# Layer 1 of a two-layer graph network: seven weights of interleaving moved from the slice steps to the scan, and two small products moved ahead of the decay's

## The chip, the cores and the metric

The kernel runs as one program on one NeuronCore of a Trainium2 chip. The metric is the device time of one execution in microseconds (us). The time before is 4291.2 us, the median of three runs (4290.76 to 4305.48 us). The profile was taken from one further execution.

## The reference, cut to what matters

`x` is 32 graphs of 512 nodes with 256 features, `adj` their adjacency. Two layers run one after the other. Layer 0 and the fall-back path of the kernel are not touched by the change. Layer 1 is an attention over the graph, and then a token mixer:

```python
# --- layer 1 ---
x = x + _L1_gnn_ref(_layernorm(x), adj, ...)      # graph attention, 4 heads of 64
x = x + _L1_ffn_ref(_layernorm(x), ...)           # slices, scan, un-slicing

# inside _L1_ffn_ref, for each graph:
sw = softmax((xm @ W_slice.T + b_slice) / temp)   # 512 nodes x 8 heads x 64 slices
st = einsum('bhnc,bhng->bhgc', fx, sw) / (sw.sum(2) + 1e-05)   # 64 slice tokens of 512
ot = _hydra(st, ...)                              # two-way scan over the 64 tokens
out = einsum('bhgc,bhng->bhnc', ot, sw)           # back to the nodes
return out @ out_w.T + out_b

# inside _hydra: z, xBC, dt from one projection; a 3-tap convolution and silu on xBC;
# y = forward and backward scan with decay exp(dt * A), moved by one token, plus
y = y + x_og * repeat(x_og @ fcD_w.T + Dp, P)     # the skip
yg = y * silu(z);  yg = yg * rsqrt(mean(yg**2) + 1e-05) * norm_w
return yg @ out_w.T
```

## The kernel before, in words

**Two streams.** `layer1_plain` writes layer 1 as Python generators. `attentions()` gives the attention of all 32 graphs in small steps: `prepare` (gather of x, layer norm, transposes, the product `hp`, the rows `own`), `attention` (the tiles `att` on VectorE, then the products `avp` and `adp` on TensorE, then the transposes `dp` and `bp`), and `norm` (the head-wise layer norm of the result, called from within the next graph's attention). `mixer(g)` gives the token mixer of a pair of graphs: `slices` for each graph, `tokens`, `scan` for both together, `unslice` for each graph.

**How they are woven.** The last loop draws values from `mixer`. Each `yield n` adds n times `PACE` to a credit, and for each whole credit one step of `attentions()` is called there. `PACE` is 1.04 * 2 * (14 + 12) / 68 = 0.795, and the weights of one pair sum to 68 before and after. The weights so decide where in the mixer's program text the attention of later graphs stands. A scheduler then sorts the instructions of each engine by the program's order and by its own view of what is ready, so that a step need not end up exactly where it was called. Each engine runs its list in order.

**The scan's chain, with its lines.** `xp` L1402 (TensorE) is evicted to `xpad` L1406 (ScalarE). VectorE runs the convolution: twelve instructions for `xT` (L1418, L1420), then `sp` (L1428 to L1434), then three for `bcT` (L1418, L1420). ScalarE makes `cpad` from it (L1445). TensorE's `gp` L1491 waits for `cpad`. The step sizes `sp` go on through L1461 to L1471 to `seg` L1485 on VectorE, for which `segp` L1495 on TensorE waits. ScalarE makes `decay` from it (L1497), and VectorE multiplies it into `mix` (L1514). `xtp` L1500 (transposes of x) and `qp` L1505 (the skip's product) need only `xT`; VectorE's `dq` L1507 reads `qp`. `yp` L1521 needs `mix`. Then come `yTp` L1531, its copy L1533 (ScalarE), `oTp` L1539, its copy L1542, `vp` L1559, and `outp` L1569 with the additions L1571 (VectorE) in `unslice`.

**The slices' chain.** `x4T` transposes, `lgp` L1336 (TensorE), exponential L1337 (ScalarE), softmax L1338 to L1343 (VectorE), then `yTp` L1348 and the transposes `swp` L1353 on TensorE.

**The norm's chain.** `mu` L1294 to L1300 on VectorE, then one power L1301 on GpSimd, then `av` L1304 and the addition L1305 on VectorE. GpSimd's list also holds the gathers L1149 (four for each graph, each pair's first waiting until a tile of x has been written out), `short` L1087, the powers L30 and L31 of the layer norms, and the additions L947 and L1187.

Of the kernel before, what the change touches and what calls it, by code (L numbers as in the profile page):

```python
# [13 lines left out]
AF = mybir.ActivationFunctionType  # L14
# [8 lines left out]
NT = N // P  # L23
# [841 lines left out]
def layer1_plain(tc, ident, eps, x2s, ranks, adj, w, out, over, ps):  # L865
# [3 lines left out]
    nc = tc.nc  # L869
    B = adj.shape[0]  # L870
    SEG = B // len(x2s)
    GB = 2
# [4 lines left out]
    G = w["W_slice"].shape[0]  # L877
# [23 lines left out]
    with ExitStack() as ctx:  # L901
# [3 lines left out]
        def ctile(name, shape):  # L905
            return cst.tile(shape, F32, tag=name, name=name)
# [6 lines left out]
        def psum(tag, name):  # L913
            return ps.tile([P, N], F32, tag=tag, name=name)
# [8 lines left out]
        with tc.tile_pool(name="raw0", bufs=1, side="right") as raw:  # L923
# [12 lines left out]
            for c in range(DC):  # L936
                nc.tensor.matmul(pn[:, : 2 * AH], ones, norm2[:, c].rearrange("p i h -> p (i h)"),
                                 start=c == 0, stop=c == DC - 1)
# [6 lines left out]
        def add_rows(xt, i):  # L945

            nc.gpsimd.dma_start(xt.rearrange("p t d -> p (t d)"), added[i].partition_broadcast(P), accum_op=ALU.add)  # L947
# [31 lines left out]
        seg_l, seg_r, side = ctile("seg_l", [P, G]), ctile("seg_r", [P, G]), ctile("side", [P, 2, G])  # L979
# [126 lines left out]
        def inner(name):  # L1106
            return sb.tile([P, DI], F32, tag="inner", name=name, bufs=6)
# [8 lines left out]
        def normed(xt, xn, name):  # L1116

            mv = sb.tile([P, NT, 2], F32, tag="mv" + name[0], name=f"mv{name}")
            for t in range(NT):
                st = sb.tile([P, 6], F32, tag="st" + name[0], name=f"st{name}_{t}", bufs=4)  # L1120
                nc.vector.bn_stats(st, xt[:, t, :])
                nc.vector.bn_aggr(mv[:, t, :], st)
            rs = sb.tile([P, NT], F32, tag="rs" + name[0], name=f"rs{name}")
            deviation(nc, rs, mv[:, :, 1], eps)
            shift = sb.tile([P, NT], F32, tag="shift" + name[0], name=f"shift{name}")
            nc.vector.scalar_tensor_tensor(shift, mv[:, :, 0], -1.0, rs, ALU.mult, ALU.mult)
            for t in range(NT):
                nc.scalar.activation(xn[:, t, :], xt[:, t, :], AF.Identity, bias=shift[:, t : t + 1],
                                     scale=rs[:, t : t + 1])

        def turned(xn, tag, name, want=None):

            xnT = sb.tile([P, DC, N], F32, tag=tag, name=name, bufs=1)
            for c in range(DC):
                pt = psum("any", f"{name}p{c}")
                for t in range(NT):
                    nc.tensor.transpose(pt[:, t * P : (t + 1) * P], xn[:, t, c * P : (c + 1) * P], ident)
                nc.scalar.copy(xnT[:, c, :], pt)  # L1138
                if c + 1 < DC:
                    yield want  # L1140
            return xnT
# [177 lines left out]
        def slices(b, j, yT, rn):  # L1319


            while b not in attended:
                next(ahead)
            xt = xs[b]
            xn = sb.tile([P, NT, D], F32, tag="xn", name=f"x4{b}", bufs=1)
            normed(xt, xn, f"d{b}")
            yield 5
            xnT = yield from turned(xn, "x4T", f"x4T{b}", 1)
            add_rows(xt, 1)
            sw = sb.tile([P, NT, DI], F32, tag="sw", name=f"sw{b}", bufs=1)  # L1330
            swT = sb.tile([P, KC, N], F32, tag="swT", name=f"swT{b}")
            yield 2
            for t in range(NT):
                pf = psum("any", f"lgp{b}_{t}")
                for c in range(DC):
                    nc.tensor.matmul(pf, xnT[:, c, t * P : (t + 1) * P], wsl[:, c, :], start=c == 0, stop=c == DC - 1)  # L1336
                nc.scalar.activation(sw[:, t, :], pf, AF.Exp)  # L1337
                nc.vector.tensor_mul(sw[:, t, :], sw[:, t, :], ebsl)  # L1338
                s = sw[:, t, :].rearrange("p (h g) -> p h g", h=H)
                st = sb.tile([P, H], F32, tag="sst", name=f"sst{b}_{t}")  # L1340
                nc.vector.tensor_reduce(st, s, AX.X, ALU.add)  # L1341
                nc.vector.reciprocal(st, st)
                nc.vector.tensor_mul(s, s, st.unsqueeze(2).to_broadcast([P, H, G]))  # L1343
                yield 5 if t + 1 == NT else 1
            for c in range(DC):
                py = psum("any", f"yTp{b}_{c}")
                for t in range(NT):
                    nc.tensor.matmul(py, xn[:, t, c * P : (c + 1) * P], sw[:, t, :], start=t == 0, stop=t == NT - 1)  # L1348
                nc.scalar.copy(yT[:, c, :, j, :], py.rearrange("p (h g) -> p h g", h=H))
            for k in range(KC):  # L1350
                pt = psum("any", f"swp{b}_{k}")
                for t in range(NT):
                    nc.tensor.transpose(pt[:, t * P : (t + 1) * P], sw[:, t, k * P : (k + 1) * P], ident)  # L1353
                nc.scalar.activation(swT[:, k, :], pt, AF.Identity, accum_out=rn[:, j, k : k + 1])
            nc.vector.tensor_scalar_add(rn[:, j, :], rn[:, j, :], 1e-5)
            nc.vector.reciprocal(rn[:, j, :], rn[:, j, :])
            return swT
# [26 lines left out]
        def scan(g, uT):  # L1384
# [4 lines left out]
            def chunks(t):  # L1389
                return t.rearrange("p (k n) -> p k n", k=KC)  # L1390
# [8 lines left out]
            for k in range(KC):  # L1399
                for c in range(KC):  # L1400
                    x0 = 2 * H + DI + k * P
                    nc.tensor.matmul(px[:, k * T : (k + 1) * T], inT[:, c, x0 : x0 + P], uT[:, c, :],  # L1402
                                     start=c == 0, stop=c == KC - 1)
# [70 lines left out]
            def heads(t):  # L1474
                return t.rearrange("p (h l) -> p h l", h=H)

            def per_head(a):
                return a.unsqueeze(2).to_broadcast([P, H, G])

            def per_slice(a):  # L1480
                return a.unsqueeze(1).to_broadcast([P, H, G])

            seg = [inner(f"seg{g}_{j}") for j in range(GB)]
            for j in range(GB):
                nc.vector.tensor_mul(heads(seg[j]), per_head(la[:, j, :]), per_slice(seg_r))  # L1485
            yield 7

            pg = psum("any", f"gp{g}")
            for i in range(2):
                for j in range(GB):  # L1490
                    nc.tensor.matmul(pg[j * G : (j + 1) * G, i * G : (i + 1) * G], bcT[:S, j, :],  # L1491
                                     cpad[:, j, 2 * i : 2 * i + G], start=True, stop=True)
            pl = psum("any", f"segp{g}")
            for j in reversed(range(GB)):
                nc.tensor.matmul(pl[j * G : (j + 1) * G, :], seg_l, seg[j], start=True, stop=True)  # L1495
            decay = inner(f"decay{g}")
            nc.scalar.activation(decay, pl, AF.Exp)  # L1497
            pt = psum("any", f"xtp{g}")
            for k in range(KC):
                nc.tensor.transpose(pt[:, k * P : (k + 1) * P], chunks(xT)[:, k, :], ident)  # L1500
# [2 lines left out]
            pq = psum("any", f"qp{g}")  # L1503
            for c in range(KC):
                nc.tensor.matmul(pq[:, :H], chunks(xT)[:, c, :], fcT[:, c, :], start=c == 0, stop=c == KC - 1)  # L1505
            q = sb.tile([P, H], F32, tag="dq", name=f"dq{g}")
            nc.vector.tensor_add(q, pq[:, :H], skip)  # L1507
            gm = sb.tile([P, 2, G], F32, tag="gm", name=f"gm{g}", bufs=1)
# [4 lines left out]
            nc.vector.tensor_add(mix, mix, back)  # L1513
            nc.vector.tensor_mul(mix, mix, decay)  # L1514

            yield 7
            py = psum("any", f"yp{g}")
            for h in range(H):
                for j in range(GB):
# [5 lines left out]
            nc.vector.tensor_add(y, y, py)  # L1525
            nc.vector.tensor_mul(y, y, z)
            ms = sb.tile([P, 1], F32, tag="ms", name=f"ms{g}")
            yield 5
            pt = psum("any", f"yTp{g}")
            for k in range(KC):  # L1530
                nc.tensor.transpose(pt[:, k * P : (k + 1) * P], y[:, k * P : (k + 1) * P], ident)  # L1531
            yT = inner(f"yT{g}")
            nc.scalar.copy(yT, pt)  # L1533
            nc.scalar.activation(z, y, AF.Square, accum_out=ms)
            yield 2
            po = psum("any", f"oTp{g}")
            for k in range(KC):
                for c in range(KC):
# [8 lines left out]
                    nc.vector.tensor_scalar(rms[i * G : (i + 1) * G, j : j + 1], ms[j * G : (j + 1) * G], 1.0 / DI, LN_EPS,  # L1547
                                            ALU.mult, ALU.add)
            nc.gpsimd.tensor_tensor(rms, rms, eps[:, 1:2].to_broadcast([P, GB]), ALU.pow)
            yield 2  # L1550

            v = sb.tile([P, NT, DI], F32, tag="sw", name=f"v{g}", bufs=1)
            v = v.rearrange("p t d -> p (t d)").rearrange("p (j k d) -> p j k d", j=GB, k=KC)
# [10 lines left out]
        def unslice(b, swT, v):  # L1564
            xt = xs.pop(b)
            for t in range(NT):
                po = psum("any", f"outp{b}_{t}")
                for k in range(KC):
                    nc.tensor.matmul(po[:, :D], swT[:, k, t * P : (t + 1) * P], v[:, k, :],  # L1569
                                     start=k == 0, stop=k == KC - 1)  # L1570
                nc.vector.tensor_add(xt[:, t, :], xt[:, t, :], po[:, :D])  # L1571
            nc.sync.dma_start(out[b].rearrange("(t p) d -> p t d", p=P), xt)
            stored.add(b)

        def mixer(g):
            uT = sb.tile([P, KC, GB * G], F32, tag="uT", name=f"uT{g}", bufs=1)
            yT = sb.tile([P, DC, H, GB, G], F32, tag="yT", name=f"yT{g}", bufs=1)
            rn = sb.tile([P, GB, KC], F32, tag="rn", name=f"rn{g}")
            sws = []
            for j in range(GB):  # L1580
                sws.append((yield from slices(g * GB + j, j, yT, rn)))
            yield 3
            tokens(g, yT, rn, uT)
            v = yield from scan(g, uT)
            yield 2
            for j in range(GB):
                unslice(g * GB + j, sws[j], v[:, j])
                yield 2


        ahead = attentions()
# [649 lines left out]
```

## Time and profile before

| | us |
|---|---|
| runs | 4305.48, 4290.76, 4291.2 (median 4291.2) |
| the profiled execution, its own time | 4294.7 |
| its span, first to last instruction | 4293.0 |
| TensorE busy | 3772.2 (88%) |
| VectorE busy | 3183.1 (74%) |
| ScalarE busy | 2105.0 (49%) |
| GpSimd busy | 1576.3 (37%) |
| first `xp` (scan of the first pair) | starts at 2498.9 |
| last `xp` (scan of the sixteenth pair) | starts at 4226.7 |

Layer 0 fills the first half of the span. From about 2400 us on only layer 1 runs, and from the first `xp` on one pair of graphs follows the other. Busy time is the time in which an engine has an instruction; matmuls are pipelined, so that a busy TensorE is not one at its peak. A row of the timeline gives start, time to the last end, engine, line, operation, output and inputs, and the count of merged records; in square brackets stands the idle time before it and what ended it. One matmul of the program is two records or more there. "PEclk" is the granted clock of TensorE as a share of full speed.

### The profile page before, as it was taken

What the parts mean: (1) busy time and instruction counts of PE and PEld (TensorE: products, weight loads), DVE (VectorE), ACT (ScalarE), POOL (GpSimd) and SP (SyncE); (2) the same over time, 40 slices, a digit from 0 to 9 for tenths busy, and PEclk for the clock granted to TensorE, in tenths of its full rate; (3) what the DMA queues carried; (4) which work ended last, traced back from release to release, by engine and by line L of the source; (5) the groups of instructions that cost most, each with busy time, mean ns of one, the idle gap of its engine ahead of it and who ended that gap; (6) DMA issues with size and microseconds to landing.
All of it is one profiled execution on the core that took longest, in us unless ns stands there. A gap on an engine that the chain in (4) does not pass through costs nothing. (4 is left out here: it accounts for less than half of the span.)

```text
span 4293.0 us, 54585 instructions
## 1 busy us (share of the span) xinstructions
PE 3772.2 (88%) x19031; PEld 2392.6 (56%) x19031; DVE 3183.1 (74%) x6973; ACT 2105.0 (49%) x4260; POOL 1576.3 (37%) x1973
## 2 busy tenths in 40 slices
PE   5567998989999999888998789999999999999997
PEld 4454565665655666554555255555555555555555
DVE  6668877888778987777775777777777777777663
ACT  3344655556556666555665344444443444444432
POOL 2345643564435644354332322223222223222210
PEclk8778999999999999999999899999999999999998
DMA  4557654575546754386542332323322333232210
GB/s 131 166 159 223 192 164 138 174 222 158 161 135 186 222 165 138 115 266 190 160 145 66 82 74 71 75 64 79 69 71 73 79 79 79 65 74 65 60 30 16
DMA packets 313244, 523.95 MB, mean 122 GB/s; under 512 B 104535, under 2 KB 196324, under 8 KB 312957
## 3 DMA queue, kind: packets, MB, share of 16 engines
q0 software_dynamic: 129408, 383.06, 32.1%
q1 hardware_dynamic: 183548, 137.29, 10.9%
q8 instruction: 152, 2.49, 0.2%
q14 instruction: 136, 1.11, 0.1%
HBM read 463.10 MB, written 73.95 MB: 125 GB/s over the span
## 5 line engine op out<-in xcount | busy, mean ns | idle before, releaser
L623 PE MATMUL clsp<-xnT,wc 128*128 128x512 f32 x1024 | 517.2, 623 | 35.0 <-ACT cls L625 30.7
L623 PE MATMUL gatep<-xnT,wg 128*128 128x512 f32 x1024 | 498.5, 606 | 19.7 <-ACT gate L625 19.6
L652 PE MATMUL po<-wd,acc 128*128 128x256 f32 x2048 | 455.4, 381 | 6.4 <-DVE acc L641 5.2
L652 PEld LDWEIGHTS po<-wd,acc 128*128 128x128 f32 x2048 | 388.9, 191 | 72.8 <-issue 9.8
L1211 DVE SCALAR_TENSOR_TENSOR att<-own,other,mask 128x512 f32<-128x512 f32 x512 | 364.5, 741 | 61.6 <-DMA own<-ownd 60.2
L599 DVE SCALAR_TENSOR_TENSOR best<-rows,xs,best 128x1024 f32<-128x1024 f32 x212 | 271.2, 1281 | 128.0 <-ACT best L593 70.0
L637 DVE SCALAR_TENSOR_TENSOR acc<-past,fld,acc 128x512 f32<-128x512 f32 x448 | 332.8, 745 | 28.8 <-ACT past L636 20.6
L623 PEld LDWEIGHTS gatep<-xnT,wg 128*128 128x128 f32 x1024 | 196.5, 196 | 262.0 <-issue 199.8
L632 ACT ACTIVATE acc<-tz,fld 128x512 f32<-128x512 f32 x256 | 199.1, 778 | 276.9 <-PE tz L630 247.0
L596 POOL DMA_INDIRECT rows<-table,xs x212 | 258.4, 1219 | 181.7 <-DVE best L599 114.3
L636 ACT ACTIVATE past<-tz,fld 128x512 f32<-128x512 f32 x448 | 291.0, 695 | 68.0 <-DVE acc L637 67.2
L1248 PE MATMUL avp<-att,hv 128*32 128x512 f32 x2048 | 260.7, 611 | 26.7 <-DVE att L1211 26.7
L1149 POOL DMA_INDIRECT x<-x2s,ranks x128 | 151.9, 1186 | 344.2 <-DVE x L1571 128.5
L623 PEld LDWEIGHTS clsp<-xnT,wc 128*128 128x128 f32 x1024 | 182.0, 198 | 169.4 <-issue 111.5
L435 PE MATMUL pm<-h,adj 128*128 128x258 f32 (+1 forms) x1024 | 180.0, 322 | 100.1 <-DVE keep L428 37.7
L1348 PE MATMUL yTp<-sw,x 128*128 128x512 f32 x512 | 242.0, 613 | 28.3 <-DVE sw L1343 28.0
L554 POOL DMA_INDIRECT xs<-rows_of,order x128 | 158.3, 1237 | 264.1 <-DVE acc L637 98.4
L625 ACT ACTIVATE gate<-gatep,fld 128x512 f32<-128x512 f32 x256 | 175.8, 687 | 156.3 <-PE gatep L623 133.8
L1301 POOL TENSOR_TENSOR mu<-mu,eps 128x16 f32<-128x16 f32 x32 | 112.0, 3499 | 361.5 <-DVE mu L1300 361.4
L1336 PE MATMUL lgp<-wsl,x4T 128*128 128x512 f32 x512 | 239.1, 610 | 1.9 <-ACT x4T L1138 1.8
L1569 PE MATMUL outp<-v,swT 128*128 128x256 f32 x1024 | 227.7, 380 | 0.0
L435 PEld LDWEIGHTS pm<-h,adj 128*128 128x128 f32 x1024 | 150.4, 211 | 124.6 <-issue 73.5
(580 smaller groups left out, 8227.4 us busy)
## 6 DMA issues: line engine op xcount, KB each, us to landing
adj<-in_adj POOLq DMA_DIRECT2D x128, 256.0 KB, 5.1
x<-added POOLq DMA_DIRECT2D x64, 512.0 KB, 5.2
own<-ownd SPq DMA_DIRECT2D x128, 256.0 KB, 3.7
rows_of<-keep SPq DMA_DIRECT2D x32, 550.0 KB, 3.9
x<-in_x SPq DMA_DIRECT2D x32, 512.0 KB, 5.3
xs<-bd POOLq DMA_DIRECT2D x32, 512.0 KB, 6.2
x2s<-xs SPq DMA_DIRECT2D x32, 512.0 KB, 2.9
short<-in_adj POOLq DMA_DIRECT2D x32, 512.0 KB, 6.0
```

The source lines that it names most:

```text
L435: nc.tensor.matmul(pm[:, : c1 - c0], a[:, i, t * P : (t + 1) * P], h[:, i, c0:c1], start=i + c0 == 0, stop=i + 1 == NT and c0 > 0)
L596: nc.gpsimd.indirect_dma_start(out=row, out_offset=None, in_=table, in_offset=bass.IndirectOffsetOnAxis(ap=idxs[:, k : k + 1].bitcast(U32) ...
L599: nc.vector.scalar_tensor_tensor(m, row, vals[:, k : k + 1], m, ALU.add, ALU.max)
L623: nc.tensor.matmul(pf, wf[:, c, f * P : (f + 1) * P], xnT[:, c, :], start=c == 0, stop=c == DC - 1)
L636: nc.scalar.activation(r, z, AF.Relu, bias=fld[:, f, AT + b : AT + b + 1])
L637: nc.vector.scalar_tensor_tensor(y, r, fld[:, f, CH + b : CH + b + 1], y, ALU.mult, ALU.add)
L652: nc.tensor.matmul(po[:, i, :], acc[f][:, t * P : (t + 1) * P], wd[:, f, :], start=f == 0, stop=f == FC - 1)
L1211: nc.vector.scalar_tensor_tensor(e, own[h], other[:, j, h : h + 1], mask[:, j, :], ALU.max, ALU.mult)
L1248: nc.tensor.matmul(pv[p][k * HW : (k + 1) * HW, :], hv[:, j, h, e : e + HW], weighed[b, h, j], **ends)
L1336: nc.tensor.matmul(pf, xnT[:, c, t * P : (t + 1) * P], wsl[:, c, :], start=c == 0, stop=c == DC - 1)
L1348: nc.tensor.matmul(py, xn[:, t, c * P : (c + 1) * P], sw[:, t, :], start=t == 0, stop=t == NT - 1)
L1569: nc.tensor.matmul(po[:, :D], swT[:, k, t * P : (t + 1) * P], v[:, k, :], start=k == 0, stop=k == KC - 1)
```

## The change

Seven of the 68 weights per pair are taken from `slices` (three in each of two graphs) and `unslice` (one) and given to `scan`. In `scan`, the transposes `xtp` with their copy and the product `qp` are written ahead of `segp` and `decay`. No instruction is added or removed.

```diff
@@ slices @@
             normed(xt, xn, f"d{b}")
-            yield 5
+            yield 3
...
-                yield 5 if t + 1 == NT else 1
+                yield 4 if t + 1 == NT else 1
@@ scan @@
                 nc.vector.tensor_mul(heads(seg[j]), per_head(la[:, j, :]), per_slice(seg_r))
-            yield 7
+            yield 9
 
             pg = psum("any", f"gp{g}")
...
-            pl = psum("any", f"segp{g}")
-            for j in reversed(range(GB)):
-                nc.tensor.matmul(pl[j * G : (j + 1) * G, :], seg_l, seg[j], start=True, stop=True)
-            decay = inner(f"decay{g}")
-            nc.scalar.activation(decay, pl, AF.Exp)
             pt = psum("any", f"xtp{g}")
...
             for c in range(KC):
                 nc.tensor.matmul(pq[:, :H], chunks(xT)[:, c, :], fcT[:, c, :], start=c == 0, stop=c == KC - 1)
+            pl = psum("any", f"segp{g}")
+            for j in reversed(range(GB)):
+                nc.tensor.matmul(pl[j * G : (j + 1) * G, :], seg_l, seg[j], start=True, stop=True)
+            decay = inner(f"decay{g}")
+            nc.scalar.activation(decay, pl, AF.Exp)
             q = sb.tile([P, H], F32, tag="dq", name=f"dq{g}")
...
             nc.vector.tensor_mul(mix, mix, decay)
 
-            yield 7
+            yield 8
             py = psum("any", f"yp{g}")
...
             ms = sb.tile([P, 1], F32, tag="ms", name=f"ms{g}")
-            yield 5
+            yield 6
             pt = psum("any", f"yTp{g}")
...
             nc.scalar.activation(z, y, AF.Square, accum_out=ms)
-            yield 2
+            yield 4
             po = psum("any", f"oTp{g}")
...
             nc.gpsimd.tensor_tensor(rms, rms, eps[:, 1:2].to_broadcast([P, GB]), ALU.pow)
-            yield 2
+            yield 3
@@ mixer @@
                 unslice(g * GB + j, sws[j], v[:, j])
-                yield 2
+                yield 2 if j else 1
```

## The prediction

> **What bounds it now.** I read the busy slices first, then the stretches of 100 us, then TensorE's waits in the stretch of full pairs, then single timelines. From 2500 to 4100 us TensorE is busy 90 to 95% of each 100 us and VectorE 66 to 77%, so TensorE's list sets the pace. Its waits from the first `xp` (2498.9) to 4115 are these:
>
> ```profile
> PE oTp L1539 <- ACT yT L1533: 26.2, 14, 1.9
> PE yTp L1348 <- DVE sw L1343: 25.9, 20, 2.3
> PE segp L1495 <- DVE seg L1485: 23.4, 13, 2.6
> PE gp L1491 <- ACT cpad L1445: 22.6, 14, 2.5
> PE vp L1559 <- ACT oT L1542: 9.4, 14, 0.7
> PE yTp L1531 <- DVE y L1526: 7.2, 14, 0.5
> PE yp L1521 <- ACT ht L1182: 6.4, 9, 0.7
> ```
>
> With 1.7 us of smaller ones that is 122.8 us in 14 pairs, 8.8 us of a pair's 116.4 us (2498.91 to 4128.31, by 14). More than this idle time, and the clock lost after it, the change can't win there. The tenth pair's rows on TensorE show where it lies; its `xp` starts at 3548.38:
>
> ```profile
> 3561.73 0.45 PE L1491 MATMUL gp<-cpad,bcT 64*64 64x64 f32 x8 [1.47 <-ACT cpad L1445]
> 3566.72 1.08 PE L1495 MATMUL segp<-seg,seg_l 128*64 128x512 f32 x4 [1.83 <-DVE seg L1485]
> 3572.66 1.15 PE L1521 MATMUL yp<-xk,mix 64*64 64x64 f32 x32 [0.71 <-ACT ht L1182]
> ...
> 3578.02 5.46 PE L1539 MATMUL oTp<-yT,hoT 128*128 128x128 f32 x32 [1.88 <-ACT yT L1533]
> ...
> 3621.84 5.55 PE L1348 MATMUL yTp<-sw,x 128*128 128x512 f32 x12 [1.39 <-DVE sw L1343]
> ```
>
> What decides below is VectorE's wait for GpSimd's power. First the scan, then the slice behind it, then the last one of the run, where VectorE has nothing else to do:
>
> ```profile
> 3551.92 1.23 DVE L1304 TENSOR_TENSOR av<-av,mu 128x1024 f32<-128x1024 f32 x1 [1.49 <-POOL mu L1301]
> 3554.86 0.48 DVE L1418 TENSOR_SCALAR xT<-xpad,conv_w 128x128 f32<-128x128 f32 x2
> ...
> 3612.53 1.23 DVE L1304 TENSOR_TENSOR av<-av,mu 128x1024 f32<-128x1024 f32 x1 [3.87 <-POOL mu L1301]
> ...
> 4161.29 0.17 DVE L1300 TENSOR_SCALAR mu<-mu 128x16 f32<-128x16 f32 x1
> 4164.47 1.22 DVE L1304 TENSOR_TENSOR av<-av,mu 128x1024 f32<-128x1024 f32 x1 [3.01 <-POOL mu L1301]
> ```
>
> ```profile
> 3548.07 3.81 POOL L1301 TENSOR_TENSOR mu<-mu,eps 128x16 f32<-128x16 f32 x1 [18.66 <-DVE mu L1300]
> ...
> 4161.54 2.90 POOL L1301 TENSOR_TENSOR mu<-mu,eps 128x16 f32<-128x16 f32 x1 [2.89 <-DVE mu L1300]
> ```
>
> And the clock, in stretches of 1 us around `oTp` at 4043.14 (time, busy, granted clock, DMA share, GB/s):
>
> ```profile
> 4042.00:4043.00 1.00, 0.00 (x0) 1.00 0.00 0
> 4043.00:4044.00 1.00, 0.86 (x4) 0.55 0.00 0
> 4044.00:4045.00 1.00, 1.00 (x6) 0.50 0.12 24
> ```
>
> **The weights: where the steps land.** I laid the built order of the changed program beside the old one. On TensorE little moves. From `zp` to `gp` there stood eight transposes, eight `avp` and four `adp` (0.97 + 1.74 + 0.96 us by starts, to 3560.26); now four transposes, four `adp`, eight `avp`, four `adp` and four `avp` (0.5 + 0.96 + 1.74 + 0.96 + 0.88, to 3561.6). From `yTp` to `oTp` still only `minep` stands, so the wait of 1.88 us stays though the weight there doubles; `dp` and `bp` now stand after thirteen of the sixteen `vp`, too late for the wait of 0.68 us. Four `adp` more in the scan, about 1 us, is all that TensorE gets of the seven weights.
>
> On VectorE much moves: the norm's tail. Before, L1300 to L1305 stood ahead of the convolution. Now in 13 of 15 pairs L1294 to L1302 stand ahead of it, and L1300 and L1304 directly behind `xT`, ahead of `sp` and `bcT`; L1305 stands between two taps of `bcT`. In the order of the engine, `sp`, `bcT`, `cpad` and so `gp` now queue behind L1304's wait.
>
> **`gp`, worked in the tenth pair.** `uT` ends at 3547.81. Ahead of the convolution now: L1294 0.08, `att` 0.66, L1295 1.14, two `att` 1.33, L1299 1.13, L1302 1.14, together 5.5, so it starts at 3553.3 (`xpad` is evicted at 3552.84) instead of 3554.86, and its 2.9 us end at 3556.2. L1300 to L1304 takes 3.18 us where VectorE idles (4161.29 to 4164.47) and 4.11 where it is busy (3547.81 to 3551.92); VectorE idles here, so 3.18. L1304 runs at 3559.4, and `sp` starts after its 1.13 at 3560.5 instead of 3558.40: 2.1 late. L1305 (1.14) in place of one BN_STATS and one aggregate (0.42) adds 0.7. `gp` becomes ready 2.8 later, at 3564.55, TensorE is free at 3561.6: a wait of 2.95 instead of 1.47, **+1.5 per pair**. In the two pairs where L1300 stands ahead of the convolution it comes to about +0.4, which the gain at `yp` below takes back. Bounds: 4.11 for the power gives +2.4, a power already done gives -1.5.
>
> **`segp`, `xtp` and `qp`.** From `gp` to `segp` was 4.99 us. More statistics now stand between `bcT` and `gm`, and the power L31 behind them ends some 0.5 later: 5.5. TensorE's work in between is 0.38 + 0.5 + 0.81 + 0.88 + 0.96 = 3.53, so about 1.97 is lost instead of 1.83: **+0.15**. The moved products replace `avp` rather than the wait. A new wait comes with them: `dq` L1507 now stands between L1461 and L1462, so `seg` queues behind `qp`. At full clock `qp` is done 1.7 after `gp`, ahead of L1461 (2.35), and costs nothing. At half clock (0.69 for `gp` at 2514.19; 1.12 and 1.71 for `xtp` and `qp` at 4244.90) it is done 3.2 to 3.5 after `gp`, and `seg` is 1.0 late. I take **+0.5**, the middle.
>
> **The clock.** After idle of 0.52 and 1.88 us around `yTp` L1531 the granted clock is 0.50 for about 3.4 us in most pairs, and `oTp` takes 5.46 instead of 3.84; after 2.55 at the first `gp` (2514.19) it fell too. 14 such stretches of 1.7 us each lie between 2499 and 4115: nine at `oTp`, three at L1348, two at `gp`. A gap of 2.95 will bring one at `gp` in nearly each pair. It falls on the 3.53 us of work ahead of `segp`, and its 1.7 us fill the 1.97 us that `segp` waits anyway; I count nothing beyond the 0.5. [...]
>
> **`yp`.** `xk` and `dq` are ready early, so `mix` follows `seg` at once, and TensorE has transposes and six `hp` (3.3) after `segp`: the 0.71 goes, as in the fifth and sixth pair, where transposes also stood there and no wait shows. `decay` now stands ahead of the `x3T` copy on ScalarE and may hold `hp` by 0 to 0.4. **-0.5**.
>
> **First slice.** The additions L1571 and the norm's tail meet: L1304 still waits, now for a power that stands behind four gathers L1149 (5.6 us from 3599.11) and `short` (0.6). Counted from the first `outp`: fourth addition done 7.5, its write-out lands 3.7 later, gathers and `short` 6.2, power 2.95: L1304 at 20.4, softmax 4.25 later at 24.65; `lgp` starts at 18.0. That is 6.65 behind `lgp`, as against 7.0 now (3606.67 to 3613.67), and L1305 stands ahead rather than inside. The wait comes to 1.5 instead of 1.85 on the average of 14 pairs: **-0.35**, and of three half-clock stretches there I take two as gone, -3 in all (0 to -5).
>
> **The end.** In the last scan `qp` comes only after `segp`, and VectorE waits 4.11 us for it (L1507, 4247.56). Moved ahead, `mix` can be done at about 4246.7 instead of 4250.3: -3.5. The pair before gains about 1.3, and the `uT` waits of 1.3 go.
>
> **Sum.** 13 x (1.5 + 0.15 + 0.5 - 0.5) = 21.5; -0.35 x 14 = -4.9; -3; -4.8 at the end; -1.3. Together **+7.5 us**. The profiled execution (4294.7, span 4293.0, 3.5 above the median) would become 4302; the median of 4291.2 about **4298**. 0.5%, 21.5 us, is about what a measurement of this kernel can tell from no change, so I forecast no change.
>
> **Rivals.** *Faster: the power is early.* If `mu` is there when L1304 is reached, `sp` starts earlier than before and `gp` never waits: 13 x 2.95 = 38 less, 4260. For it speaks that VectorE gains 1.5 us ahead of the convolution, and that the weights sit where TensorE waits; against it, 3 us or more behind each L1300 in all rows of L1304. *Slower: a second half-clock stretch.* `gp` waits 2.95 and `segp` up to 1.97 within 9 us. If the clock falls for both, the second stretch lies on `segp`, `hp` and `yp`, where no wait takes it up: 13 x 1.7 = 22, 4320. It decides once a second gap of about 1.9 us falls in one stretch; the last scan shows it, at 0.50 nearly throughout from 4241 to 4262. *The weights do nothing*, since the scheduler sorts them away: 4286, only the end's gain. I count that as no change.
>
> **Chances.** No change 0.47 (4276 to 4312), faster 0.27, slower 0.26. The range goes from 4260 to 4320 and leaves out less than 2 in 10: both ends are the rivals' own times.
>
> **What would show it.** Right: L1304 with idle of about 3 us behind `xT` in some 13 scans; `gp`'s waits at 35 to 45 us instead of 22.6; no wait at `yp`; `oTp`'s and `vp`'s waits unchanged; half clock just behind `gp`; L1348 at about 20 us; no wait of `dq` in the last scan. Wrong: `gp` waiting less than before, L1304 without a wait in the scan, or new waits in the second slice, where fewer weights stand.

## The result, and the profile after

The changed kernel takes 4345.84 us (median of four runs, 4335.97 to 4348.50), the kernel before on the same chip 4292.8 us (median of four, 4290.76 to 4305.48): a ratio of 1.0113, 95% interval 1.0087 to 1.0139. It is slower by 53 us, where the prediction said 4298 us and no change. The profiled execution has a span of 4346.4 us instead of 4293.0.

First the waits of TensorE in the changed kernel, in the same stretch as before the change (columns: the waiting product, its releaser, us in total, times, longest):

```profile
PE gp L1491 <- ACT cpad L1445: 36.0, 13, 3.1
PE yTp L1348 <- DVE sw L1343: 27.8, 26, 3.3
PE oTp L1539 <- ACT yT L1533: 26.8, 14, 2.1
...
PE hp L1176 <- ACT x3T L1138: 4.5, 8, 0.7
PE segp L1503 <- DVE seg L1485: 1.5, 3, 0.8
```

The sum of all waits has become smaller, not larger: from the first `xp` to the fifteenth 113.9 us instead of 122.7. `gp` waits 36.0 us instead of 22.6, `segp` 1.5 instead of 23.4, and `yp` not at all. So the loss isn't in the waits. The tenth pair on TensorE shows a part of it (`xp` starts at 3587.42):

```profile
3603.65 0.69 PE L1491 MATMUL gp<-cpad,bcT 64*64 64x64 f32 x8 [3.06 <-ACT cpad L1445]
3604.27 1.11 PE L1495 MATMUL xtp<-ident,xT 128*128 128x128 f32 x4
3605.18 1.71 PE L1500 MATMUL qp<-fcT,xT 128*128 128x8 f32 x8
...
3609.97 1.08 PE L1503 MATMUL segp<-seg,seg_l 128*64 128x512 f32 x4
...
3625.04 3.23 PE L1559 MATMUL vp<-owT,oT 64*64 64x256 f32 x26 [0.68 <-ACT oT L1542]
...
3629.23 1.07 PE L1559 MATMUL vp<-owT,oT 64*64 64x256 f32 x6
```

`gp` waits 3.06 us, and behind it the products take up to twice their time: `qp` 1.71 us instead of 0.96. The clock around it, in stretches of 3.41 us (start and end, length, busy time of TensorE, granted clock, DMA share, GB/s):

```profile
3599.26:3602.68 3.42, 1.32 (x16) 1.00 0.00 0
3602.68:3606.09 3.41, 2.44 (x17) 0.50 0.00 0
3606.09:3609.50 3.41, 3.41 (x20) 0.50 0.00 0
3609.50:3612.92 3.42, 3.03 (x20) 1.00 0.75 140
```

Half clock follows a stretch that is 39% busy and lasts two such stretches, 6.8 us. What TensorE does in them takes twice its time (eight records of `avp` 1.71 us by starts from 3606.82 on, 0.86 at full clock from 3596.97 on), so that half of the busy time is lost. VectorE's timeline of the same pair shows where the gap comes from:

```profile
3598.44 1.23 DVE L1304 TENSOR_TENSOR av<-av,mu 128x1024 f32<-128x1024 f32 x1 [3.07 <-POOL mu L1301]
3599.58 0.17 DVE L1428 TENSOR_TENSOR sp<-bcp,dtb 128x16 f32<-128x16 f32 x1
...
3606.93 0.17 DVE L1507 TENSOR_TENSOR dq<-qp,skip 128x8 f32<-128x8 f32 x1 [0.86 <-PE qp L1500]
```

L1304 stands behind the convolution of x and ahead of `sp`, and waits 3.07 us for the power.

I split the time from the first `xp` to the fifteenth (fourteen pairs) into idle time (gaps of over 0.15 us), time lost to half clock (half of the time in which TensorE is busy at half clock), and the rest, which is TensorE's own work. The same split is used for the experiments, each from one profiled execution. "Windows" counts the stretches of 3.41 us at half clock; each costs up to 1.71 us.

| kernel | first `xp` | 14 pairs | idle | of it `gp` | lost to half clock (windows) | TensorE's own |
|---|---|---|---|---|---|---|
| before | 2498.9 | 1629.4 | 122.7 | 22.6 | 23.6 (14) | 1483.1 |
| changed | 2508.1 | 1674.2 | 113.9 | 36.0 | 58.1 (36) | 1502.2 |
| weights_only | 2511.1 | 1700.1 | 127.7 | 36.0 | 72.2 (46) | 1500.2 |
| reorder_only | 2504.1 | 1614.9 | 96.7 | 22.3 | 36.3 (22) | 1481.9 |
| after_norm_behind_mix | 2505.5 | 1620.6 | 92.1 | 0.6 | 18.2 (12) | 1510.3 |
| after_products_ahead_of_gp | 2497.9 | 1653.0 | 119.7 | 27.3 | 32.4 (20) | 1500.9 |
| after_late_weights_back | 2498.1 | 1651.8 | 104.7 | 35.7 | 53.5 (33) | 1493.6 |
| before_warm_oTp | 2505.7 | 1616.4 | 106.5 | 22.3 | 6.8 (4) | 1503.1 |
| before_gp_stalled | 2501.0 | 1687.4 | 143.0 | 55.9 | 63.9 (45) | 1480.5 |
| reorder_gp_stalled | 2508.2 | 1675.2 | 129.1 | 55.5 | 64.7 (41) | 1481.4 |
| reorder_qp_behind_segp | 2503.3 | 1635.5 | 113.7 | 22.5 | 36.9 (22) | 1484.9 |

The changed kernel's 53.4 us are 44.8 us in the fourteen pairs (idle -8.8, clock +34.5, own work +19.1), +9.2 us ahead of the first `xp`, +3.9 in the fifteenth pair and -4.5 from the last `xp` on. The 9.2 us I can't ascribe to the change: the first `xp` of all fifteen profiled kernels lies between 2497.9 and 2517.8, and the run after_products_ahead_of_gp, with the same weights, has it at 2497.9.

### The profile page after: what moved, and what is told of

The parts are those of the page before. It is cut to its first block, busy times and chain, and to the rows that moved or that the text cites. A ratio compares the mean times of both kernels' runs of the same rounds, so it can differ in the third digit from the quotient of the medians.

```text
span 4346.4 us, 54603 instructions
## 1 busy us (share of the span) xinstructions
PE 3820.1 (88%) x19031; PEld 2407.3 (55%) x19031; DVE 3173.2 (73%) x6973; ACT 2119.6 (49%) x4260; POOL 1557.2 (36%) x1973
## 5 line engine op out<-in xcount | busy, mean ns | idle before, releaser
L1248 PE MATMUL avp<-att,hv 128*32 128x512 f32 x2048 | 283.1, 629 | 21.3 <-DVE att L1211 20.9
L1348 PE MATMUL yTp<-sw,x 128*128 128x512 f32 x512 | 243.3, 620 | 28.0 <-DVE sw L1343 27.8
L625 ACT ACTIVATE cls<-clsp,fld 128x512 f32<-128x512 f32 x256 | 176.4, 689 | 77.9 <-PE clsp L623 50.7
```

Source lines behind the costliest of these rows:

```text
L625: nc.scalar.activation(o, pf, fn, bias=fld[:, f, bf : bf + 1], scale=1.0 if fn == AF.Gelu else 0.5)
L1248: nc.tensor.matmul(pv[p][k * HW : (k + 1) * HW, :], hv[:, j, h, e : e + HW], weighed[b, h, j], **ends)
```

## The experiments

They ran on four chips, on which the kernel before took 4307 to 4312 us (medians), so the ratios to it are what counts; the changed kernel's is 1.0113 from its own chip. The theory: the weights put L1304's wait ahead of `sp`, the gap at `gp` grows to 3 us, and the clock falls behind it. Rival A: the moved products cost the time. Rival B: TensorE changes more often between different products, which costs time by itself.

**The two parts alone.** weights_only has only the changed `yield` numbers; reorder_only has only the second edit of the diff, the five lines of `segp` and `decay` behind `qp`.

> Only the weights of the change; xtp and qp stay behind segp. Theory: with the new weights the first part of the even graph's norm (L1291 to L1297) is called from the yield behind the convolution's text instead of from the one ahead of xp, so L1304 with its wait for GpSimd's power lands ahead of sp and bcT, gp waits about 3.1 us in most scans (36 us in 14 pairs), and the clock falls for two windows (6.8 us) there. It expects nearly all of the loss: 4335 to 4355 us, gp's waits at 33 to 40 us, 20 or more windows of half clock between the first and the last xp. Rival A, the moved products (dq holding seg, xtp and qp run at half clock): 4285 to 4310 us. Rival B, finer mixing of different products on TensorE: also 4330 to 4350, but with time per instruction, not the clock, carrying it.

> Only xtp, xk and qp ahead of segp and decay; weights as before. Theory: gp's waits stay at about 1.5 us per pair, so no new half-clock stretch; the last scan's dq wait goes, 3 to 5 us: 4280 to 4300 us. Rival A: 4320 us or more. Rival B: no change in mixing, 4285 to 4295 us.

weights_only: 1.0145 (1.0118 to 1.0173). reorder_only: 0.9913 (0.9887 to 0.9939). The waits of weights_only, and then of reorder_only:

```profile
PE gp L1491 <- ACT cpad L1445: 36.0, 13, 3.1
...
PE segp L1495 <- DVE seg L1485: 19.1, 12, 2.2
```

```profile
PE gp L1491 <- ACT cpad L1445: 22.3, 14, 2.5
...
PE segp L1503 <- DVE seg L1485: 5.5, 8, 1.5
```

The weights alone lose at least as much as the whole change (the two intervals overlap): the same 36.0 us at `gp`, and 46 windows of half clock. The order alone is a gain of 0.9%, far more than the 3 to 5 us expected: `segp`'s wait falls from 23.4 to 5.5 us and the 6.4 us at `yp` go, with nothing added to `gp`'s wait. So the moved products aren't the source of the loss. The change is a gain and a larger loss in one. The parts don't add, though: on top of the new weights the order brings only 0.3% (1.0145 to 1.0113), which isn't clear of the noise.

Rival A is right about the clock all the same. No new stretch of half clock was expected of reorder_only, but it has 22 windows instead of 14, seven of them behind `gp` instead of two. And `gp`'s gap is the same in weights_only as in the changed kernel, only what runs behind it differs. First the changed kernel's eleventh pair, with `qp` behind `gp`, then the tenth pair of weights_only, where products of the attention stand there:

```profile
3718.73:3722.14 3.41, 0.34 (x8) 1.00 0.00 0
3722.14:3725.55 3.41, 3.41 (x24) 0.50 0.02 5
3725.55:3728.97 3.41, 3.41 (x18) 0.50 0.08 12
```

```profile
3625.51:3628.93 3.41, 0.35 (x10) 1.00 0.00 0
3628.93:3632.34 3.41, 3.41 (x24) 0.50 0.01 2
3632.34:3635.75 3.41, 2.06 (x15) 1.00 0.27 38
```

In both the gap lies in one window and the next is fully busy at half clock. With 1.71 us of `qp` in it, another one at half clock follows; without `qp` the clock comes back. (`xtp` was moved along with it, but in before_warm_oTp below, with twelve transposes of its shape, 1.47 us, ahead of `oTp`, no half clock is left there.) In the changed kernel the first half-clock window behind `gp` was followed by another in eleven of twelve scans, in weights_only in five of twelve, and in those five it was only 49 to 88% busy. What weights_only saves there is lost elsewhere: `segp` still waits 19.1 us, and the windows of half clock are 46 instead of 36 in all.

**The gap taken away.** after_norm_behind_mix adds one edge of order to the changed kernel:

```diff
-            nc.vector.tensor_mul(heads, heads, mu...)                # L1304
+            tail = nc.vector.tensor_mul(heads, heads, mu...)
+            if gate:                     # set behind mix L1514, cleared ahead of yp
+                behind(tail, gate[0])
```

> The changed kernel with one ordering edge more: L1304 of the norm called in the scan is issued behind the last instruction of mix (L1514) on VectorE, so it no longer stands ahead of sp and bcT. Theory: gp's wait falls from 3.06 us to under 0.5 and the 6.8 us of half clock behind it go in 13 scans; about 2.9 us of idle and 2.4 us of lost clock per pair, of which 1 us may come back at segp or yp: 13 x 4.3 = 56 us, so about 4290 us, and half-clock windows fall to about 15 between the first and the last xp. Rival A: stays at 4330 or more. Rival B, finer mixing: 18 us of the loss stay, 4305 to 4320 us.

Ratio 0.9968 (0.9954 to 0.9983), 1.4% below the changed kernel's 1.0113. Its waits:

```profile
PE vp L1562 <- ACT oT L1545: 27.8, 14, 4.1
...
PE gp L1493 <- ACT cpad L1447: 0.6, 1, 0.6
```

`gp` waits 0.6 us in fourteen pairs, and the windows of half clock fall from 36 to 12. So L1304's place carries the loss at `gp` and the clock behind it: 35 us of idle and 40 us of clock. A part comes back as a new wait of `vp` (27.8 us), because a layer norm that follows the moved instructions (four of L1128, 2.07 us in the tenth pair) now runs on ScalarE just ahead of the copy of `oT`. And TensorE's own time stays high (1510 us, against 1483 before), which is rival B's part.

**The gap filled.** after_products_ahead_of_gp has `xtp`, `xk` and `qp` written ahead of `gp` in the changed kernel, with no new instruction.

> The changed kernel with xtp, xk and qp written ahead of gp, so that their 1.3 us of TensorE work fill part of the gap that gp waits in. Theory, a gap of more than about 1.85 us inside one of the clock's windows of 3.41 us puts the next window at half clock: gp's wait falls from 3.06 to about 1.7 us, under that bound, and most of the 6.8 us stretches behind gp go: per pair 1.4 us of idle and 2.4 to 3.4 us of clock less, 1.5 us back at segp, 13 x 2.5 = about 33 us: ratio 1.001 to 1.006 to before, instead of 1.0113. Rival A, the small products run at half clock are what prolongs the stretch: they are gone from behind gp too, so only the gap's length tells: with stretches of 3.4 us still there in most scans it was the products, with none it was the gap. Rival C, the gap costs only its own length: 18 us, ratio 1.007.

Ratio 1.0043 (1.0025 to 1.0061). `gp`'s wait shrinks only to 2.4 us in most pairs, not to the 1.7 us expected, but the windows go from 36 to 20. In seven of the twelve scans in which `gp` waits the clock still falls right behind it, each time for one window and never for two. By the expectation's own terms that points to the small products as what prolongs the stretch, though the gap is 0.7 us shorter too. The loss in clock is 26 us smaller, and 0.9 to 2.6 us of idle come back at `segp` in most pairs.

**The late weights.** after_late_weights_back undoes three of the weights:

```diff
-            yield 4
+            yield 2
             po = psum("any", f"oTp{g}")
...
-            yield 3
+            yield 2
             v = sb.tile([P, NT, DI], F32, tag="sw", ...)
...
             v = yield from scan(g, uT)
-            yield 2
+            yield 5
```

> The changed kernel with the two last raised weights put back (ahead of oTp 4 to 2, ahead of vp 3 to 2) and their three given to the yield behind vp (2 to 5); the sum stays 68. In the built order dp and bp then stand behind the sixteen vp and no longer between them; the rest of the scan is the same. Rival B, finer mixing costs TensorE time of its own: vp goes back from 4.17 to 3.6 us per pair and the whole run gains 8 us, ratio about 1.009. Theory, only the gap at gp and the clock: no change, 1.0113, gp's waits at 36 us, half clock as in the changed kernel.

Ratio 1.0033 (1.0017 to 1.0048), 0.8% better than the changed kernel, where rival B had 0.2% and the theory nothing. `vp` is one block again:

```profile
3605.53 3.67 PE L1559 MATMUL vp<-owT,oT 64*64 64x256 f32 x32 [0.68 <-ACT oT L1542]
```

Counted by starts, without idle and with half clock taken out, `vp` takes 3.6 us per pair again and not 4.17; in fourteen pairs 7.5 of the 8.6 us by which TensorE's own work shrinks. The waits of L1348 fall from 27.8 to 20.6 us, since the norm's parts come at other places in the first slice. Rival B holds for a part of the loss, and `vp`'s share is as large as it said. The profile gives 22 us in the pairs (9 of them idle, 5 clock), the ratios 34 us; the remainder lies ahead of the first `xp`, where the runs scatter by as much.

**The gap alone.** before_gp_stalled and reorder_gp_stalled put a power of their own in the chain of `bcT`, with the weights as before:

```diff
+            wait = sb.tile([P, 12], F32, tag="wait", name=f"wait{g}", bufs=1)
+            nc.vector.tensor_scalar_max(wait, v[:, :12], 1.0)
+            nc.gpsimd.tensor_tensor(wait, wait, eps[:, 1:2].to_broadcast([P, 12]), ALU.pow)
+            nc.vector.tensor_copy(bcT[:, 0, :12], wait)
             conv(bpad, bc_w, bcT)
```

> The kernel before, weights and order as before, with a power of 128x12 on GpSimd put into the chain of bcT: VectorE waits for it (a copy into bcT that the convolution overwrites) where L1304 waits in the changed kernel. By the powers of 128x4 (1.0 us) and 128x16 (2.9 us) it lasts about 2.3 us, and gp should wait 2.7 to 3.3 us instead of 1.5. It makes the gap alone, with no mixing and with xtp and qp behind segp. Theory, the gap costs its length and one window of half clock (3.4 us) at gp: 1.6 + 1.7 less 0.4 back at segp, 14 x 2.9 = 40 us, ratio about 1.009. Rival C, only its length: 14 x 1.2 = 17 us, ratio 1.004.

> The same power in the chain of bcT, with xtp, xk and qp ahead of segp: the gap and the moved products together, without the new weights. Rival A, the small products xtp and qp in the first half-clock window hold the clock down for a second one: stretches of 6.8 us at gp in most scans, 1.6 + 3.4 less about 0.5, 14 x 4.5 = 63 us over the order alone (0.9913): ratio about 1.006. If the length of the gap decides, as many stretches of 3.4 us as in the run with the old order beside it: ratio about 0.9985 to 1.001.

Ratios 1.0105 (1.0075 to 1.0135) and 1.0120 (1.0089 to 1.0150). The gap came out longer than the 2.7 to 3.3 us expected: 3.1 to 5.2 us in both, 3.6 in six of the fourteen pairs. With no change of weights it makes a loss as large as the change's. In the fourteen pairs of before_gp_stalled that is 58 us: 33 more at `gp`, 40 of clock, 13 less in other waits, and TensorE's own work about as before. Rival C, only the gap's length, would have been 1.004. Behind the stalled `gp` of before_gp_stalled the clock reads:

```profile
3604.55:3607.96 3.41, 1.25 (x16) 1.00 0.00 0
3607.96:3611.37 3.41, 1.94 (x12) 0.50 0.00 0
3611.37:3614.79 3.42, 3.36 (x12) 0.50 0.80 152
```

Two windows here too, although `xtp` and `qp` come later: the second wait, 1.53 us of `segp`, leaves the first window at half clock only 57% busy, and it is followed by another. So a second wait can do what `qp` does. In the changed kernel it isn't the second wait, since `segp` hardly waits there. With the products ahead, half clock at `gp` lasts two windows or more in 13 of 14 scans, against 12 of 14 without them, so that this pair of kernels can't tell the two causes apart; the stall cost all of the order's gain and 1.2% more, above what either expectation had.

**The clock at `oTp`.** before_warm_oTp adds work that is overwritten, in the gap that ScalarE's copy of `yT` makes:

```diff
             po = psum("any", f"oTp{g}")
+            for k in range(12):
+                nc.tensor.transpose(po[:, k % KC * P : (k % KC + 1) * P], y[:, k % KC * P : (k % KC + 1) * P], ident)
```

> The kernel before with twelve more transposes of y into the bank of oTp, ahead of its products, which overwrite them: TensorE is busy while ScalarE copies yT, and no real product starts earlier. Theory, that a gap costs its own length and then a window of half clock: the 9 half-clock stretches of 1.7 us behind yTp go, about -15 us, 4275 us, with oTp at 3.8 us instead of 5.5 us. Rival: the clock falls for other reasons (power, overall load), and nothing changes within 5 us, or the extra work makes it slower by up to 10 us.

Ratio 0.9965 (0.9952 to 0.9979), 15 us, as expected. The added transposes and the products behind them:

```profile
3575.01 1.47 PE L1538 MATMUL oTp<-ident,y 128*128 128x128 f32 x12
3577.05 3.84 PE L1541 MATMUL oTp<-yT,hoT 128*128 128x128 f32 x32 [0.56 <-ACT yT L1533]
```

The products take 3.84 us and not 5.46, and start no earlier relative to `y`. Of 14 windows of half clock 4 are left, none of them at `oTp`. That a gap costs the clock behind it is shown by this run alone, with the other waits nearly as before.

**Two tries for a better version, and `qp`.** reorder_norm_behind_seg is reorder_only with L1304 behind `seg` (the edge as above, set at L1485); combined_order_fences_warm adds an edge for the first slice (behind L1343) and the twelve transposes; order_and_warm is reorder_only with the transposes alone.

> The order of the change with the weights of before, and one ordering edge: L1304 called in the scan is issued behind seg (L1485). Theory: gp's remaining 1.5 us per pair go, in part back at yp: 10 to 20 us better than the order alone (0.9913), so 0.987 to 0.990, with gp's waits under 5 us in all. Rival: mix comes 2.3 us later behind the norm's tail and yp waits for it: no gain, 0.991 to 0.994.

> The order of the change, the weights of before, both ordering edges (L1304 of the scan behind seg, L1304 of the first slice behind the slice's last softmax product L1343) and the twelve extra transposes ahead of oTp. Theory, gaps and clock windows: gp's 1.5 us, L1348's 1.4 us and nearly all half clock between the first and the last xp go: 4205 to 4240 us on the first chip, ratio 0.978 to 0.988, with at most 5 half-clock windows. Rival: second slices wait instead, since their x is normed 10 us later: 0.988 to 0.995.

> The order of the change with the weights of before, and the twelve extra transposes of y ahead of oTp; no ordering edges. Theory, the two gains add: 0.9913 and 0.9965, ratio 0.986 to 0.989, half-clock windows between the first and the last xp under 8. Rival, the clock's windows fall elsewhere once the pair is shorter: 0.990 to 0.993.

0.9929 (0.9900 to 0.9958), 0.9890 (0.9863 to 0.9917) and 0.9896 (0.9869 to 0.9923). `gp` doesn't wait any more with the edge, but `yp`, L1531 and `oTp` then do (8.1, 17.5 and 29.1 us, against 0, 7.3 and 26.1 in reorder_only), as the rival said: moving the norm's tail behind `seg` brings nothing. Both edges together with the transposes come out just above the theory's 0.988 and in the rival's range, with 8 windows of half clock instead of 5, and are no better than the order and the transposes alone. For these two alone the gains would multiply to 0.988, which lies in the interval of 0.9896: they add, as far as the noise lets one see. The last two kernels ask what `qp` does to the clock. reorder_qp_behind_segp moves only `xtp` and `xk` ahead of `segp`; before_products_ahead_of_gp_warm has the weights of before, the three ahead of `gp`, and the transposes.

> The order alone, but with only xtp and xk ahead of segp; qp goes back behind it. Theory, qp with its 8 columns keeps TensorE busy by the record but does not count for the clock: in the run with the whole order six windows fell to half clock although they were 53 to 69% busy, all of them with qp, and those falls go; any window that still falls from full clock is under 0.47 busy. In time it is a wash, 8 windows of 1.7 us less against 0.8 us more wait at segp in 14 pairs: ratio 0.988 to 0.993. Rival, the falls come from the gaps at gp and segp alone, whatever runs between: windows of 0.5 to 0.7 busy still fall, as often as before.

> The weights of before, xtp, xk and qp ahead of gp, between products of the attention, and the twelve extra transposes ahead of oTp. Theory: gp's wait of 1.5 us falls under 0.4 and segp's rises to about 1; no window behind gp falls, and between the first and the last xp half clock is left only at L1348, 0 to 4 windows. Against the order with the transposes (0.9896) 0.8 us of idle in 14 pairs and about 10 us of clock: ratio 0.982 to 0.987. Rival, xtp and qp only move the wait to segp: 0.988 to 0.992.

0.9982 (0.9968 to 0.9997) and 0.9898 (0.9880 to 0.9915). The first was a miss: not a wash but 0.7% worse than the whole order, since `segp` waits 16.2 us instead of 5.5 and `yp` 5.1 us again. It says that most of the order's gain comes from `qp` as work in `segp`'s gap. The windows of half clock stay at 22. Three windows that hold `qp` still fell, now at `segp` and 63% busy, and two of 49 and 53% fell without it. The second confirmed its rival: the wait moved from `gp` (0.2 us) to `segp` (13.6 us) and `xtp` (7.8 us). All three kernels with order and transposes lie at 0.989 to 0.990, about 1.1% below the kernel before and 2.2% below the changed one.

## Why the prediction was wrong, by its own steps

The terms of its sum beside what the profiles show (us; rounded, so that the columns add to within 0.1):

| term | forecast | measured |
|---|---|---|
| `gp`'s wait | +19.5 | +13.4 |
| `segp`'s wait and `dq`, with the clock at `gp` beyond it | +8.5 | +12.4 (wait -21.9, clock +34.3) |
| `yp` and `hp` | -6.5 | -1.9 |
| first slice: wait at L1348, its clock | -4.9, -3 | +1.9, +4.1 |
| clock at `oTp` | 0 | -3.9 |
| other waits, `uT`'s among them | -1.3 | -0.3 |
| TensorE's own work | 0 | +19.1 |
| fifteenth pair | -1.3 | +3.9 |
| from the last `xp` on | -3.5 | -4.5 |
| ahead of the first `xp` | 0 | +9.2 |
| sum | +7.5 | +53.4 |

**`gp`: right.** It said L1304 would wait about 3 us behind `xT` in some 13 scans and `gp` 2.95 us, 35 to 45 us in all. Measured: 3.07 us at L1304 in eleven of the fourteen scans, 2.5 to 3.1 us at `gp` in twelve, 36.0 us in all; two scans have no wait at L1304. The rise is 13.4 us and not 19.5, since these two scans wait 0.5 us or less at `gp`, and the wait before was 1.6 us on the average and not 1.47. The new wait of `dq` for `qp` at half clock is there too (0.86 us in the row above).

**The clock: this step failed.** The prediction let the clock fall at `gp` in each pair, counted one window of 1.7 us, and wrote that "its 1.7 us fill the 1.97 us that `segp` waits anyway; I count nothing beyond the 0.5". The fill is real: `segp`'s wait fell by 21.9 us. But in eleven of the twelve scans with a fall the stretch is two windows, 6.8 us: 11 x 3.4 + 1.7 = 39 us of half clock against 22 us filled. In seven of the eleven the gap lies wholly ahead of the first half-clock window, which is fully busy and holds 0.9 to 1.7 us of `qp`. In the other four a part of the gap, 0.6 to 1.0 us, spills into that window, as in the tenth pair, and it is 71 to 81% busy and holds 0.9 to 1.2 us of `qp`. The twelfth scan has no `qp` in its first half-clock window, and no second one. The slower rival put the second stretch at 22 us and made it depend on a second gap; here `qp`, in four scans with the spill, did it without one. That the terms of `gp`, `segp` and the clock together still come near their forecast (25.8 us against 28.0) is luck: `gp`'s wait grew by less and `segp`'s went, which hides the second window.

**TensorE's own work: this step failed as well, and it is the largest term.** The prediction read the new order for cover, said "On TensorE little moves", and put nothing for it. The same products took 19.1 us more in fourteen pairs: `vp` +0.57 us per pair where `dp` and `bp` stand in it, the transposes of x3T and x4T +0.52, `avp` and `adp` +0.65, `bp` +0.14, less 0.5 in other products, clock taken out of each. The last six records of `vp` above take 1.0 us by starts, against 0.68 in an unbroken block (6/32 of 3.6). It comes with the weights: weights_only has it (1500 us), reorder_only hasn't (1482). after_late_weights_back shows `vp`'s share to be due to the split of its block; that the other shares come from more frequent changes of product in the same way is likely, but not shown.

**`yp`, `oTp`, `vp`: right.** `yp`'s 6.4 us went, the hold of `hp` by the x3T copy is 4.5 us (predicted 0 to 0.4 per pair), `oTp` and `vp` wait 26.8 and 9.5 us as before. **First slice: wrong.** L1348 was to go to 20 us and lose two windows; it has 27.8 us, and six windows instead of three, 14 us off in the sum. L1304 waits about 4.44 us there in eight of fourteen pairs, where 3.87 was the most frequent wait. **The end: half right.** The wait of `dq` in the last scan fell from 4.11 to 1.09 us and the time from the last `xp` on by 4.5 us, but the fifteenth pair lost 3.9 us: L1304 waits 3.05 us there too, `gp` 2.6 us instead of 1.1, and one more window is at half clock.

The order's own worth was missed as well: it was entered as "+0.15" at `segp`, because the order was only ever looked at with the new weights. By itself it is worth 0.9%, and the new weights on top of it cost 2% (1.0113 against 0.9913).

## What to carry to other kernels

Count a gap on TensorE at its length plus the clock behind it, and place it in the clock's windows: here, of 243 windows at full clock that were under 47% busy, 218 were followed by one of half clock, at up to 1.71 us each. A second one came where the gap spilled into the first or another wait fell into it (all 43 that were under 80% busy), or where small products such as `qp` filled it (all 34 that were fully busy with 0.83 us or more of `qp`). Two waits that look separate (here `gp` and `segp`) are then one problem, and what runs behind a gap matters as well as its length. When weights or priorities decide where steps land, look in the built order for an instruction that waits for another engine (here L1304, 3.07 us for GpSimd's power) and for what now stands behind it, and count how often TensorE changes product, not only how much cover it has (here `vp` took 4.17 us per pair in a split block and 3.6 in one). And take a change with two parts apart before judging it: here one part was worth 0.9% and the other cost 1.4%.

## What the runs showed of the clock

In each of the fifteen profiled kernels every change of the granted clock between 2480 us and the fifteenth `xp`, 498 in all, lies on one grid of 3.4133 us, within 0.01 us; the grid's phase differs from execution to execution. The windows are the steps of this grid. By the share of a window in which TensorE has an instruction, in all these executions (2500 us to the fifteenth `xp`): at full clock all 152 windows under 0.40 busy are followed by half clock, 66 of 91 between 0.40 and 0.47, 5 of 25 between 0.47 and 0.50, 20 of 371 between 0.50 and 0.70, and none of 6,225 above. At half clock all 43 windows under 0.80 busy are followed by another one; above that 51 of 294 are.

Busy by the record isn't all that counts. Of the fully busy windows at half clock, all 167 without `qp`, whose products have 8 columns, were followed by full clock. Of the 59 with `qp`, all 22 that hold up to 0.75 us of it rose too, and all 34 that hold 0.83 us or more stayed, as did one of the three between. Of the 20 windows that fell although 50 to 70% busy, 18 hold `qp`, against 40 of all 371. The window at 2634.73 of reorder_only is 64% busy (2.18 of 3.41 us), with 0.96 us of `qp` in it, and the next one is at half clock:

```profile
2634.73:2638.14 3.41, 2.18 (x24) 1.00 0.00 0
2638.14:2641.56 3.42, 3.42 (x20) 0.50 0.00 0
```

Why windows with `qp` fall or stay at half clock when others of the same busy time don't, no run here measured by itself; it stays open.
